# A sparse layer's experts, one at a time or two to a block, in a transformer layer on one core

## The chip, the core and the metric

The kernel runs on one core of a Trainium2 chip. The metric is device time in microseconds (us) of one execution, and the kernel before took 3014.79 us (median of three runs, 3014.07 to 3015.65). A core has a matrix engine (PE, with its weight loads shown apart as PEld), a vector engine (DVE), an activation engine (ACT), a general engine (POOL) and a queue that only issues transfers (SP). PE multiplies a stationary operand, loaded into its 128 x 128 array, by a moving one that streams through, and writes to PSUM, eight banks of 512 floats on each of 128 partitions. DVE and ACT carry results from there to SBUF. Transfers run on 16 DMA engines. Each engine works through its own queue in order and waits on semaphores for the others.

## The reference, cut to what matters

```
x = L0_attn_x                          # (8, 1024, 256) float32, 8192 tokens
x = x + 0.5 * ffn(layernorm(x))
x = x + attention(layernorm(x))        # 16 heads of 16
x = x + 0.5 * ffn(layernorm(x))

def ffn(input):                        # E = 8 experts, C = 320 places, D = 256, H = 1024
    xf = input.reshape(N, D)
    eid = argmax(softmax(xf @ router_w + router_b))
    rank = (number of earlier tokens of the same expert)
    valid = rank < C
    buf[eid, rank] = xf                # where valid
    h = relu(einsum('ecd,edh->ech', buf, w1) + b1)
    y = einsum('ech,ehd->ecd', h, w2) + b2
    yov = relu(xf @ ow1 + ob1) @ ow2 + ob2
    return y[eid, rank] where valid, else yov
```

Each expert takes the first 320 tokens that choose it. All later ones go through one shared network of the same shape, ow1 and ow2. Everything is float32.

## The kernel before, in words

Both feed-forwards are an object of the class `Layer`. Routing (`route`, `places`) normalizes a batch, finds each token's expert and rank, and scatters its row into a DRAM buffer, `buf`: 8 x 320 rows for the experts, then all tokens past them. A row has 256 values and the token's number.

`blocks` (lines 427 to 488) then works on blocks of rows, one after the other. A block of an expert has 320 rows, held as tiles of 128, 128 and 64; a shared block has 512, four tiles. For each block:

- `load` (411) has the rows on their way from `buf` (`load_rows`, 402, on SP). POOL copies out the token numbers (416) and gathers each token's old value into `old` (419, an indirect transfer that POOL issues).
- `transposed` (192) turns rows to columns: two transposes a tile on PE into PSUM (199), and one copy by ACT of the whole (204).
- The hidden layer is computed transposed. The 1024 hidden units are eight groups of 128, taken two at a time into a tile of two PSUM banks (`big`, two such tiles). For each group two matmuls (445) have a piece of w1 stationary and the block's columns moving: 320 columns for an expert, 512 for a shared block. ACT evicts the first bank of the two with bias and relu (455), DVE the second (458).
- DVE adds the halved second bias to the old values (467).
- For each tile, eight matmuls (473) accumulate the output: a piece of the hidden layer (128 hidden units by n tokens) is stationary, w2's rows (128 x 256) move. For an expert's third tile n is 64, so half of the array's columns have work.
- DVE evicts it as y, half of the product plus old (480), and POOL scatters y to the tokens' places (483).

The next block's transposes stand ahead of the present block's last tile (470), so that ACT's copy lies beside that tile's matmuls.

`expert` (491) makes a block for `blocks`: it loads the expert's second bias, b2, to all partitions (496), has POOL halve it (497), calls `load`, and loads w1 (`wa`, 501) and w2 (`wb`, 502) on SP, 1 MB each. `wa`, `wb` and `bb` have two buffers, so an expert's weights load while the one before computes.

The order on PE, ACT and DVE is that in which the program is written (`manual_schedule`). The order on POOL and SP is made by the framework, and both queues run in order. The framework places waits where a tile's buffer is used again, and also where a new pool's tile lies in memory on an older pool's tile.

`feed_forward` (590) runs the stages: shared blocks beside routing, then the eight experts in a pool of their own (633), then further shared blocks. The first feed-forward has its last shared blocks run beside the first steps of attention, the second runs two shared blocks after the experts.

Attention runs between the two (`attention`, 703). Of it this matters: for two batches in turn, the values stand in the tiles `vp0` and `vp1` (742), 8768 bytes of every partition each, in which ones beside the values give the softmax's sums. They lie in the pool `const`, open for the whole kernel, and POOL fills both with ones at the kernel's start. `weigh` (964) multiplies them: for each of four heads one matmul with 32 stationary columns, written to its own 32 PSUM partitions, so each head has its own quarter of the array's columns.

Of the kernel before, what the change touches and what calls it, by code (L numbers as in the profile page):

```python
# [40 lines left out]
def macaron(  # L41
# [12 lines left out]
    def big(name):  # L54
        return psum["big"].tile([P, 1024], F32, tag="big", name=name)
# [27 lines left out]
    def load(name, src, shape, pool=const):  # L83
        t = pool.tile(shape, F32, tag=name, name=name)
        nc.scalar.dma_start(out=t, in_=src)
        return t
# [105 lines left out]
    def transposed(pool, tag, name, rows):  # L192

        width = sum(n for _, n in rows)
        ps = big(f"pt_{name}").rearrange("p (k c) -> p k c", k=KC)
        at = 0
        for r, n in rows:
            for k in range(KC):
                nc.tensor.transpose(  # L199
                    ps[:, k, at : at + n], r[:n, k * P : (k + 1) * P], ident[:n, :n]  # L200
                )
            at += n
        to = pool.tile([P, KC, width], F32, tag=tag, name=name)
        nc.scalar.copy(to, ps[:, :, :width])  # L204
        return to
# [35 lines left out]
    class Layer:  # L241
# [169 lines left out]
        def load(self, pool, name, at, count, weights, bias, after):  # L411

            rows, olds = self.rows.pop(at, None) or self.load_rows(pool, name, at, count), []
            ids = pool.tile([P, WIDE // P], I32, tag="ids", name=f"ids_{name}")
            for i, (r, n) in enumerate(rows):
                nc.gpsimd.tensor_copy(ids[:n, i : i + 1], r[:n, D : D + 1].bitcast(I32))
                old = pool.tile([P, D], F32, tag="old", name=f"old_{name}_{i}")

                nc.gpsimd.indirect_dma_start(
                    out=old[:n, :], out_offset=None, in_=self.old,  # L420
                    in_offset=bass.IndirectOffsetOnAxis(ap=ids[:n, i : i + 1], axis=0),
                    bounds_check=N - 1, oob_is_err=False,
                )
                olds.append(old)
            return name, rows, ids, olds, weights, bias, after

        def blocks(self, pool, those, late=False):

            those = iter(those)
            one, xnt = next(those, None), None
            while one is not None:
                name, rows, ids, olds, (wa, wb), bias, after = one
                width = sum(n for _, n in rows)
                if xnt is None:
                    xnt = transposed(pool, "xet", f"bT_{name}", rows)
                    yield
                following = None if late else next(those, None)
                hs = []  # L440
                for m in range(0, MC, 2):
                    ps = big(f"ph_{name}_{m}")
                    for i in range(2):
                        for k in range(KC):
                            nc.tensor.matmul(  # L445
                                ps[:, i * 512 : i * 512 + width],
                                lhsT=wa[:, k, (m + i) * P : (m + i + 1) * P],
                                rhs=xnt[:, k, :],
                                start=(k == 0),
                                stop=(k == KC - 1),  # L450
                            )
                        if i == 0:
                            yield
                    h = pool.tile([P, 2, width], F32, tag="he", name=f"h_{name}_{m}")
                    nc.scalar.activation(  # L455
                        h[:, 0, :], ps[:, :width], AF.Relu, bias=bias[:, m : m + 1]
                    )
                    nc.vector.tensor_scalar(  # L458
                        h[:, 1, :], ps[:, 512 : 512 + width], bias[:, m + 1 : m + 2], 0.0,
                        ALU.add, ALU.max,  # L460
                    )
                    hs += [h[:, 0, :], h[:, 1, :]]
                    yield
                if late:
                    following = next(those, None)
                for (_, n), old in zip(rows, olds):
                    nc.vector.tensor_tensor(old[:n, :], old[:n, :], after[:n, :], ALU.add)
                for i, ((_, n), old) in enumerate(zip(rows, olds)):
                    if following is not None and i == len(rows) - 1:
                        xnt = transposed(pool, "xet", f"bT_{following[0]}", following[1])  # L470
                    ps = acc(f"pe_{name}_{i}")
                    for m in range(MC):
                        nc.tensor.matmul(  # L473
                            ps[:n, :D], lhsT=hs[m][:, i * P : i * P + n], rhs=wb[:, m, :],
                            start=(m == 0), stop=(m == MC - 1),
                        )
                        if m == MC // 2:
                            yield
                    y = pool.tile([P, D], F32, tag="y", name=f"y_{name}_{i}")
                    nc.vector.scalar_tensor_tensor(  # L480
                        y[:n, :], ps[:n, :D], 0.5, old[:n, :], ALU.mult, ALU.add
                    )
                    nc.gpsimd.indirect_dma_start(
                        out=self.new.pop(0),
                        out_offset=bass.IndirectOffsetOnAxis(ap=ids[:n, i : i + 1], axis=0),
                        in_=y[:n, :], in_offset=None, bounds_check=N - 1, oob_is_err=False,
                    )
                    yield
                one = following

        def expert(self, pool, e):
            name = f"{self.f}_{e}"
            wa = pool.tile([P, KC, H], F32, tag="wa", name=f"wa_{name}")
            wb = pool.tile([P, MC, D], F32, tag="wb", name=f"wb_{name}")
            bb = pool.tile([P, D], F32, tag="bb", name=f"bb_{name}")
            nc.sync.dma_start(out=bb, in_=b2[e].partition_broadcast(P))
            nc.gpsimd.tensor_scalar(bb, bb, 0.5, None, ALU.mult)
            one = self.load(
                pool, f"e{name}", e * CAP, CAP, (wa, wb), b1_sb[:, e * MC : (e + 1) * MC], bb
            )  # L500
            nc.sync.dma_start(out=wa, in_=w1[e].rearrange("(k p) f -> p k f", p=P))
            nc.sync.dma_start(out=wb, in_=w2[e].rearrange("(m p) d -> p m d", p=P))
            return one
# [86 lines left out]
        def feed_forward(self, start, others=None, following=None):  # L590
# [13 lines left out]
            with self.pools, space(f"ffn{f}", {  # L604
                "he": 4, "old": 8, "xet": 2, "y": 4
            }, self.main, side="right") as main:
                def past(at, width=WIDE):
                    return self.load(
                        main, f"o{f}_{at}", SLOTS + at, width, self.shared, ob1_sb, ob2_sb
                    )  # L610
# [9 lines left out]
                with two_sizes(f"ps{f}", 4):  # L620
# [12 lines left out]
                    with space(f"experts{f}", {"wa": 2, "wb": 2, "bb": 2}, main, side="right") as pool:  # L633
                        with tc.manual_schedule(engines=ordered):
                            end = at if f == 0 else sure(B - 1)
                            run(self.blocks(main, chain(
                                (self.expert(pool, e) for e in range(E)),
                                (past(i * WIDE) for i in range(at, end)),
                            )))
# [63 lines left out]
    def attention(use, kept, weights, router):  # L703
# [36 lines left out]
        for i in range(2):  # L740
            vp = kept.tile([P, TB * HEADS * V + S], F32, tag=f"vp{i}", name=f"vp{i}")
            nc.gpsimd.memset(vp, 1.0)
            vps.append(vp)
# [366 lines left out]

        def zero_rows(i):
            m = use.pool.tile([P, 512], F32R, tag=f"m{i}", name=f"m{i}")
            nc.gpsimd.memset(m.bitcast(F32), 0.0)
            ms.append(m)

        def first_pair(others):
# [4 lines left out]
            for i in range(2):  # L1121
                zero_rows(i)
            zero = clearing(use.pool)
# [36 lines left out]
        def run(own):  # L1160
            for i in range(2, 4):
                zero_rows(i)
            fetch(1)
            for b in range(AHEAD - 1, B):
                reload(b)
                beside.append([G * (b - 1) - 1, DVE, stats(b)])
# [74 lines left out]
    first_pair, run = attention(use, const, weights, layers[1])  # L1241

    def beside_last(blocks, main):
# [12 lines left out]
        "q0": 1, "k0": 1, "m0": 1, "m1": 1, "zero": 1, "lowest": 2, "lowboth": 2,  # L1256
# [3 lines left out]
    with space("early", sizes) as early:  # L1260
        layers[0].feed_forward(0, fill_weights, beside_last)
        own = {
            "ex": 8, "ho": 4, "xn": 4, "xnt": 1, "q1": 1, "q2": 1, "k1": 1, "k2": 1, "ot0": 1,
# [82 lines left out]
```

## Time and profile before

| what | value |
|---|---|
| median of three runs | 3014.79 us |
| profiled execution, its own time | 3016.21 us |
| its span, first to last instruction | 3014.3 us |
| PE, DVE, ACT, POOL busy | 94%, 62%, 45%, 29% |
| first experts, hidden layer's first matmul to the next block's transposes | 375.6 to 535.0 us |
| second experts, likewise to the next block's hidden layer | 2785.6 to 2945.9 us |
| granted PE clock, mean | 0.988 |

The profile is one execution. Its views are the page (busy time; the span in 40 slices with a digit for the tenths busy; the chain that ended last; groups of instructions), a timeline of each engine's instructions with equal ones merged, a table of busy time by stretches of time, and the waits. A matmul of float32 stands in the trace as two passes, so the counts of matmuls are twice the program's. Passes overlap in the pipeline: what a pass costs is the distance from its start to the next start, and not its duration. In a timeline's line the columns are start, length, engine, line, operation, output<-inputs, shape and count, and in brackets the idle time before it.

### The profile page before, as it was taken

The page shows a single profiled execution, that of the slowest core. Times are in us where ns is not written, and L with a number is a line of the kernel's source. Part 1 is how long each engine was busy: PE and PEld are TensorE (multiplying, and loading weights), DVE is VectorE, ACT ScalarE, POOL GpSimd, SP SyncE. Part 2 cuts the span into 40 slices and gives each one's busy share as a digit, 9 for nine tenths or more (in the row PEclk, how much of TensorE's full clock was granted, in tenths as well). Part 3 has the DMA queues.
Part 4 walks back from the last instruction along what each step waited for, and adds up shares of the span by engine and source line. Part 5 has one row for each costly group of instructions (what it writes and reads, how often), then busy time and mean ns, then how long its engine had stood idle before and what let it go on. Part 6 is the DMA issues. An engine that isn't in the chain of part 4 may idle for free.

```text
span 3014.3 us, 56661 instructions
## 1 busy us (share of the span) xinstructions
PE 2846.8 (94%) x22082; PEld 1570.5 (52%) x22082; DVE 1873.6 (62%) x4155; ACT 1367.9 (45%) x2480; POOL 878.0 (29%) x1176
## 2 busy tenths in 40 slices
PE   4599999999999999999999999999999998999998
PEld 4367677554444444444444444444444445667775
DVE  5344322366898788788788788788788953222221
ACT  0011111203766765766766766766766762111110
POOL 2353443513200121421421421421410215433331
PEclk9899999999999999999999999999999999999999
DMA  8241364423211211311311311311321102311430
GB/s 216 87 125 60 98 196 126 142 80 123 93 45 38 107 45 38 121 45 38 121 45 38 121 45 38 121 45 38 121 80 38 38 3 71 124 59 54 153 123 28
DMA packets 162840, 250.41 MB, mean 83 GB/s; under 512 B 36865, under 2 KB 108802, under 8 KB 162562
## 3 DMA queue, kind: packets, MB, share of 16 engines
q1 hardware_dynamic: 143026, 195.88, 20.1%
q0 software_dynamic: 18688, 50.62, 5.0%
q8 instruction: 177, 2.90, 0.4%
q14 instruction: 101, 0.83, 0.1%
q10 hardware_dynamic: 848, 0.18, 0.0%
HBM read 143.05 MB, written 103.57 MB: 82 GB/s over the span
## 4 chain that ended last, share of the span: by engine, by line
PE 62%; DVE 13%; issue 1%; POOL 1%; DMA 0%; ACT 0%; POOLq 0%; ACTq 0%
PE psc L933 19%; PE av L964 14%; DVE halves L949 9%; PE pm L933 6%; PE pe_o L473 5%; PE ph_o L445 5%; PE pe_e L473 3%; PE ph_e L445 2%; PE pu L1009 2%; PE pxd L808 2%; PE pv L840 1%; DVE turned L979 1%; PE pq L826 1%; PE pl L1037 1%; PE ptrn L778 0%
## 5 line engine op out<-in xcount | busy, mean ns | idle before, releaser
L949 DVE TENSOR_REDUCE halves<-pm 128x1 f32<-128x512 f32 x2048 | 1308.8, 681 | 255.7 <-PE pm L933 232.4
L942 ACT ACTIVATE ex<-psc 128x512 f32<-128x512 f32 x2048 | 1111.7, 596 | 572.4 <-PE psc L933 566.7
L933 PE MATMUL pm<-k,q 32*128 32x512 f32 x4096 | 870.3, 448 | 49.6 <-DVE halves L949 38.7
L933 PE MATMUL psc<-q,k 32*128 32x512 f32 x4096 | 790.1, 454 | 3.3 <-PEq L615 3.3
L964 PE MATMUL av<-ex,vp 128*32 128x256 f32 (+1 forms) x6472 | 610.1, 448 | 0.0
L933 PEld LDWEIGHTS psc<-q,k 32*128 32x128 f32 x4096 | 326.2, 183 | 478.9 <-issue 423.3
L933 PEld LDWEIGHTS pm<-k,q 32*128 32x128 f32 x4096 | 374.8, 183 | 133.1 <-DVE halves L949 108.6
L933 PE MATMUL psc<-m,ones_r 32*128 32x512 f32 x2048 | 406.5, 390 | 0.0
L445 PE MATMUL ph_o<-bT_o,oa 128*128 128x512 f32 x704 | 325.3, 613 | 10.9 <-DVE h_o L458 7.5
L473 PE MATMUL pe_o<-ob,h_o 128*128 128x256 f32 x1408 | 324.7, 387 | 0.0
L987 POOL TENSOR_TENSOR ot<-turned,rec 128x256 f32<-128x256 f32 x64 | 39.7, 621 | 881.7 <-DVE rec L982 875.4
L473 PEld LDWEIGHTS pe_o<-ob,h_o 128*128 128x128 f32 x1408 | 268.4, 194 | 47.6 <-issue 12.9
L964 PEld LDWEIGHTS av<-ex,vp 128*32 128x32 f32 x6472 | 127.6, 108 | 297.7 <-issue 274.9
L458 DVE TENSOR_SCALAR h_o<-ph_o,ob 128x512 f32<-128x512 f32 x88 | 66.0, 750 | 253.1 <-ACT h_o L455 235.3
L445 PEld LDWEIGHTS ph_o<-bT_o,oa 128*128 128x128 f32 x704 | 133.8, 195 | 167.4 <-issue 154.1
L455 ACT ACTIVATE h_o<-ph_o,ob 128x512 f32<-128x512 f32 x88 | 60.4, 687 | 332.2 <-PE ph_o L445 264.1
L933 PEld LDWEIGHTS psc<-m,ones_r 32*128 32x128 f32 x2048 | 196.0, 184 | 12.3
L473 PE MATMUL pe_e<-wb,h_e 128*128 128x256 f32 (+1 forms) x768 | 171.7, 380 | 0.0
L480 DVE SCALAR_TENSOR_TENSOR y_o<-pe_o,old_o 128x256 f32<-128x256 f32 x88 | 37.3, 423 | 184.2 <-PE pe_o L473 158.8
L473 PEld LDWEIGHTS pe_e<-wb,h_e 128*128 128x128 f32 (+1 forms) x768 | 131.0, 172 | 34.0 <-issue 0.5
L445 PE MATMUL ph_e<-bT_e,wa 128*128 128x320 f32 x512 | 142.1, 436 | 1.6 <-issue 0.8
L204 ACT COPY bT_o<-pt_bT_o 128x1024 f32<-128x1024 f32 x22 | 22.3, 1013 | 260.5 <-PE pt_bT_o L199 260.5
(173 smaller groups left out, 2364.0 us busy)
## 6 DMA issues: line engine op xcount, KB each, us to landing
k<-krows SPq DMA_DIRECT2D x64, 512.0 KB
wa<-in_w_dram SPq DMA_DIRECT2D x16, 1024.0 KB
wb<-in_w_dram SPq DMA_DIRECT2D x16, 1024.0 KB
krows<-kh SPq DMA_DIRECT2D x32, 512.0 KB
krows<-kl SPq DMA_DIRECT2D x32, 512.0 KB
q<-qrows SPq DMA_DIRECT2D x32, 512.0 KB
rows_o<-buf SPq DMA_DIRECT2D x88, 130.0 KB
x<-in_x_dram SPq DMA_DIRECT2D x8, 1024.0 KB
```

Source lines behind the costliest of these rows:

```text
L445: nc.tensor.matmul(ps[:, i * 512 : i * 512 + width], lhsT=wa[:, k, (m + i) * P : (m + i + 1) * P], rhs=xnt[:, k, :], start=(k == 0), stop= ...
L455: nc.scalar.activation(h[:, 0, :], ps[:, :width], AF.Relu, bias=bias[:, m : m + 1])
L458: nc.vector.tensor_scalar(h[:, 1, :], ps[:, 512 : 512 + width], bias[:, m + 1 : m + 2], 0.0, ALU.add, ALU.max,)
L473: nc.tensor.matmul(ps[:n, :D], lhsT=hs[m][:, i * P : i * P + n], rhs=wb[:, m, :], start=(m == 0), stop=(m == MC - 1),)
L480: nc.vector.scalar_tensor_tensor(y[:n, :], ps[:n, :D], 0.5, old[:n, :], ALU.mult, ALU.add)
L808: nc.tensor.matmul(ps, lhsT=wd_sb[:, k, m * P : (m + 1) * P], rhs=xnt[:, k, :], start=(k == 0), stop=(k == KC - 1),)
L933: nc.tensor.matmul(ps, lhsT=lhs, rhs=rhs, start=(len(left) + 1 == todo[kind, h, "of"]), stop=not left,)
L942: nc.scalar.activation(ex, ps, AF.Exp, scale=S ** -0.5)
L949: nc.vector.tensor_reduce(halves[m][:, t, half, h : h + 1], ps, AX.X, ALU.max, negate=True)
L964: nc.tensor.matmul(avs[n, q][32 * h : 32 * h + 32, cols], lhsT=vps[b % 2][:, at : at + 2 * S], rhs=ex[:, cols], start=(c == 0), stop=(c == ...
L987: nc.gpsimd.tensor_tensor(outs_t[q][:, :, at : at + S].rearrange("p (t a) s -> p a t s", t=4), by[:, :, :S].rearrange("p (a t) s -> p a t ...
L1009: nc.tensor.matmul(ps[:, i * D : (i + 1) * D], lhsT=outs[b, g, q][:, at : at + P], rhs=wu_sb[:, g, :], start=(g == 0), stop=(g == G // 2 - 1),
```

## The change

Two experts make one block of 640 rows, held as five full tiles. Its middle tile has the first expert's last 64 rows and the second's first 64. For every hidden group the middle tile gets two matmuls of 64 stationary columns: the first expert's, with the first w2, to PSUM partitions 0 to 63, and the second's, with the second w2, to 64 to 127.

- The hidden layer is computed expert by expert, as before. The first expert's is evicted in two pieces: columns 0 to 255 into h, and the last 64 into a new tile, `kept`, as the middle tile is computed after the second expert's hidden layer.
- Order in a block: first hidden layer, additions to five olds, tiles 0 and 1, second hidden layer, the middle tile, tile 3, next transposes, tile 4.
- `transposed` works in chunks of four tiles, each with a `big` of its own and a copy by ACT, so a pair has two copies, of 1024 and 256 elements.
- The second biases of a pair are one tile of three columns of 256 (first, both by halves, second), filled by four loads, with one buffer, halved by one instruction. `old` has 10 buffers instead of 8. `wa` and `wb` keep two buffers, one for each expert of the pair.
- `vp0` moves from `const` to the pool `early` and `vp1` to attention's own pool. Each is filled with ones by POOL there, `vp0` with attention's first steps, `vp1` as attention begins in earnest.

The diff, cut to its core:

```
     def transposed(pool, tag, name, rows):
+        to = pool.tile([P, KC, sum(n for _, n in rows)], F32, tag=tag, name=name)
         at = 0
+        for c in range(0, len(rows), 4):
+            ps = big(f"pt_{name}").rearrange("p (k c) -> p k c", k=KC)
+            width = 0
+            for r, n in rows[c : c + 4]:
+                for k in range(KC):
+                    nc.tensor.transpose(
+                        ps[:, k, width : width + n], r[:n, k * P : (k + 1) * P], ident[:n, :n]
+                    )
+                width += n
+            nc.scalar.copy(to[:, :, at : at + width], ps[:, :, :width])
+            at += width
         return to
...
+                for wa, wb, bias, (c0, c1) in parts:
+                    width = c1 - c0
+                    ahead = c1 % P if c1 != parts[-1][3][1] else 0
+                    if ahead:
+                        kept = pool.tile([P, MC, ahead], F32, tag="kept", name=f"kept_{name}")
...
+                        h = pool.tile([P, 2, width], F32, tag="he", name=f"h_{name}_{c0}_{m}")
+                        pieces = [(h, c0, c1 - ahead)]
+                        if ahead:
+                            pieces.append((kept[:, m : m + 2, :], c1 - ahead, c1))
+                        for t, lo, hi in pieces:
+                            nc.scalar.activation(
+                                t[:, 0, : hi - lo], ps[:, lo - c0 : hi - c0], AF.Relu,
+                                bias=bias[:, m : m + 1],
                             )
+                            nc.vector.tensor_scalar(
+                                t[:, 1, : hi - lo], ps[:, 512 + lo - c0 : 512 + hi - c0],
+                                bias[:, m + 1 : m + 2], 0.0, ALU.add, ALU.max,
+                            )
+                        for i in range(2):
+                            hs[m + i] += [(t[:, i, :], wb, lo, hi) for t, lo, hi in pieces]
...
+                    while to_do and to_do[0] * P + rows[to_do[0]][1] <= c1:
+                        i = to_do.pop(0)
+                        n = rows[i][1]
+                        if following is not None and not to_do:
+                            xnt = transposed(pool, "xet", f"bT_{following[0]}", following[1])
+                        ps = acc(f"pe_{name}_{i}")
+                        for m in range(MC):
+                            for of, w, a, b in hs[m]:
+                                lo, hi = max(i * P, a), min(i * P + n, b)
+                                if lo < hi:
+                                    nc.tensor.matmul(
+                                        ps[lo - i * P : hi - i * P, :D],
+                                        lhsT=of[:, lo - a : hi - a],
+                                        rhs=w[:, m, :],
+                                        start=(m == 0),
+                                        stop=(m == MC - 1),
+                                    )
...
+        def ones(i):
+            vp = use.pool.tile([P, TB * HEADS * V + S], F32, tag=f"vp{i}", name=f"vp{i}")
+            nc.gpsimd.memset(vp, 1.0)
+            vps.append(vp)
```

## The prediction

> **What bounds the kernel now.** The page's busy table and its slices come first.
>
> ```profile
> PE 2846.8 (94%) x22082; PEld 1570.5 (52%) x22082; DVE 1873.6 (62%) x4155; ACT 1367.9 (45%) x2480; POOL 878.0 (29%) x1176
> ...
> PE   4599999999999999999999999999999998999998
> PEld 4367677554444444444444444444444445667775
> DVE  5344322366898788788788788788788953222221
> ```
>
> PE is busy nearly everywhere, and outside attention (the tenth to the 34th slice) nothing else is near full. The edited code is a stage of its own, in the sixth and seventh slice and again in the 38th and 39th, where DVE is at 2 tenths. The table by stretches of time gives its two runs:
>
> ```profile
> 375.60:535.00 159.40, 159.40 (x682) 118.35 (x682) 35.28 (x79) 21.71 (x39) 64.30 (x86) 1.00 0.50 157
> 2785.60:2945.90 160.30, 160.30 (x691) 119.31 (x691) 35.27 (x79) 22.73 (x40) 58.92 (x81) 1.00 0.43 137
> ```
>
> PE is busy for the whole of both (first and second number equal), at full clock; DVE works 35 us of 159, ACT 22, and DMA is half used. So only PE's own work counts here. PE's timeline shows one expert:
>
> ```profile
> 475.66 8.88 PE L445 MATMUL ph_e<-bT_e,wa 128*128 128x320 f32 x32
> 484.38 7.07 PE L473 MATMUL pe_e<-wb,h_e 128*128 128x256 f32 x32
> 491.28 0.87 PE L199 MATMUL pt_bT_e<-ident,rows_e 128*128 128x128 f32 x6
> 492.08 3.67 PE L473 MATMUL pe_e<-wb,h_e 128*64 128x256 f32 x16
> 495.68 0.54 PE L445 MATMUL ph_e<-bT_e,wa 128*128 128x320 f32 x1
> ```
>
> Durations overlap, so I take differences of starts. Each matmul of the program stands as two passes in the trace (x16 for the eight of a tile). The hidden layer takes 484.38-475.66 = 8.72 us; two full tiles 6.90 (3.45 each, 0.2156 a pass); the next expert's transposes 0.80; the half tile 3.60, as long as a full one. Sum 20.02, eight times over.
>
> **The change part by part**, made against the profiled execution (3016.21 us, span 3014.3), which stands 1.4 us above the median of the runs, 3014.79; I subtract the difference from the median.
>
> *Unchanged:* the hidden layers, 8 x 8.72 a feed-forward, and 16 full tiles of 3.45 (two of each expert before; four of each pair after): 124.96 us.
>
> *The middle tile.* Before, eight half tiles a feed-forward, 28.8 us. After, four middle tiles, each with the same 32 passes of 64 columns, but alternating between the left and the right half of the array. The trace has no such pair. The nearest row is attention's, where four groups of 32 columns get a matmul each:
>
> ```profile
> 1505.66 0.40 PE L933 MATMUL psc<-m,ones_r 32*128 32x512 f32 x2
> 1505.99 0.64 PE L964 MATMUL av<-ex,vp 128*32 128x256 f32 x8
> 1506.56 0.50 PE L933 MATMUL psc<-q,k 32*128 32x512 f32 x2
> ```
>
> Eight passes of the half tile's length fill 0.57 us to the next start; one after the other they would need 8 x 0.2156 = 1.72. The records show four starting within 0.02 us, the other four 0.240 later. All four groups write one bank and use all 128 rows, as the two halves will. So two halves should run side by side: 16 steps of 0.2156 (the half tile's pass) to 0.240 (attention's), plus what entering and leaving 64 columns costs now, 3.60-16x0.2156 = 0.15. That is 3.60 to 3.99; I take 3.75, nearer the half tile, whose width and length it has. Four: 15.0 us, a gain of 13.8 a feed-forward (12.8 to 14.4).
>
> *Transposes.* In the stage's first run, seven experts' of 0.80 (5.6 us), in the second also 0.96 of the shared block that follows. The 64-row ones cost more than full ones: the full ones start 0.11 apart, the small pair takes the last 0.36. After: ten full ones for three pairs, 3 x 1.10 = 3.3, and in the second run 0.88 (eight full ones ahead of a full tile at 2581.51). Gains 2.3 and 2.4.
>
> *Entry.* A stage's first block has no tile to hide its transposes:
>
> ```profile
> 373.93 0.87 PE L199 MATMUL pt_bT_e<-ident,rows_e 128*128 128x128 f32 x6
> 374.38 4.13 SPq L407 DMA_DIRECT2D rows_e<-buf  x1
> 374.84 0.69 ACT L204 COPY bT_e<-pt_bT_e 128x640 f32<-128x640 f32 x1 [13.83 <-PE pt_bT_e L199]
> 375.58 1.61 PE L445 MATMUL ph_e<-bT_e,wa 128*128 128x320 f32 x5 [0.78 <-issue]
> ```
>
> That is 1.65 us from transposes to hidden layer. With eight transposes and a copy of 1024 it is 2.20 (535.01 to 537.21); a second copy, of 256, costs about 0.37 by the line through 0.69 (640) and 1.01 (1024), if the matmul waits for it. Loss 0.55 to 0.92 a stage, taken as 0.75. Inside the stage the two copies (1.4 us) lie beside a full tile of 3.45.
>
> *Evictions.* The first expert's hidden layer is now evicted in four pieces, and in the new program each waits for the one before: ACT 256, DVE 256, ACT 64, DVE 64 columns. From 527 and 687 ns (ACT, 320 and 512) and 550 and 750 (DVE), the pieces are about 0.47, 0.48, 0.31 and 0.28; with 0.20 from PE to ACT and three hand-overs of 0.03, 1.83 us. The other bank pair's matmuls cover 2.18 (a quarter of 8.72), so the cost is nothing, with 0.35 us to spare. If pieces ran as long as the 320 ones, the chain would be 2.45, and two waits of 0.27 in a pair would cost 4 us in all.
>
> *Loads and queues.* With a pair at 36 us, the last weights freed with time pressing are the first expert's wb: free after the middle tile (28 us in), needed 9 us into the next pair, 17 us later. Behind that wait on SP stand the next rows, whose transposes are a pair away. A megabyte took 3.6 us at the 292 GB/s of the stretch 375.6 to 395.6. The bias tile has one buffer and four loads, free after the additions (12 us in) and needed at 45. POOL has five gathers and five scatters of 1.3 us and a scaling of 2.7 in 36. In the first pair two more row loads stand ahead of wa, 0.5 us of SP each; 8.9 us lay between wa's issue (366.70) and its first use (375.58). Cost nothing.
>
> *DVE* makes 8 additions and 8 evictions of y fewer a feed-forward; it is idle there, gain nothing.
>
> *Attention's values.* Two memsets (3.79 us of POOL at 11.9, before PE's first matmul at 20.64, which waits for DVE) become one there and one at attention's start, 1.92 us ahead of POOL's an, which ended at 727.3 while PE took it at 732.75. Nothing, or a gain of up to 0.3 at the start. Tiles move in memory, so a wait for an older tile's reader may appear or go: the one of 7.54 us on PE at 2522.9 (ACT's second h_o behind the sends) stays, as both tiles keep their places; for others I allow 2 us either way.
>
> Sum: (13.8+2.3-0.75) + (13.8+2.4-0.75) = 30.8. 3014.8-30.8 = **2984 us**; with the bounds 2980 to 2990.
>
> **The rivals.**
> *Loads exposed.* If a pass's weight load hid only behind passes of other rows, each of the 16 steps would pay it: 0.137 (the 128*64 load's row). The middle tile would be 16x0.353+0.15 = 5.8, 2.05 more, 16.4 over eight: 3000. Against it: in the half tile the next load starts 2 ns after the pass before and the passes stay 0.2156 apart; in attention the second four loads start 0.03 us after the first passes. The Trainium skill, "TensorE: Matmul & The Clock Gate", in Part 3 on packing small matmuls, says that a weight load overlaps running matmuls only when its row group differs, and both halves use every row. By that rule the time is this rival's 3000; these rows speak against it.
> *Halves one after the other*, so that the edit doesn't do what it says: 32x0.2156+0.15 = 7.05, 3.3 more a pair, 26.4 in all: 3010. Attention's row speaks against it, but with 32 columns and a single round, never sixteen.
> *Slower.* Alternating halves run in turn and each also waits for its load: 32x0.353+0.15 = 11.4 a pair, 7.7 more, 61 in all: 3045. Its place is the middle tile, and it decides from 7.6 us of middle tile (0.233 a pass), where the gain of 3.85 a pair is used up. The first rival's rows and attention's both speak against it.
>
> **How the numbers follow.** Side by side 0.80 (2984, own range 2980 to 2990), loads exposed 0.08 (3000), in turn 0.06 (3010), slower 0.04 (3045); 0.02 for a late transfer or a new wait, of either sign. 0.2% is 6 us, about what a measurement of this kernel can tell from no change. The third rival (-4) lies within it. Faster 0.88, same 0.07, slower 0.05. The range, 2979 to 3000, takes in the forecast's and reaches to the first rival.
>
> **What would show it.** Per pair, PE's timeline should have 17.4 us of hidden layer, four full tiles of 3.45, one stretch of 128*64 passes of 3.6 to 4.0 with starts in twos, and ten transposes 0.11 apart, 36.1 in all against 40.0, with PE busy throughout and attention's stretch as long as before. A middle stretch of 5.8, 7 or 11 names the rival. A PE idle ahead of ph_e waiting for DVE would show my chain of evictions too short; one waiting for wa or wb, the slack of loads.

## The result, and the profile after

The changed kernel took 2984.6 us (median of four runs, 2979.6 to 2990.4) beside 3014.4 for the kernel before: a ratio of 0.9902, 95% interval 0.9883 to 0.9921. The forecast was 2984. The profiled execution is the fastest of the four, 2979.6 us with a span of 2977.9 at a mean granted clock of 0.989.

The same lines of the page as before, now of the changed kernel: PE's row of the busy table, then the slices.

```profile
PE 2814.6 (95%) x22066; PEld 1551.4 (52%) x22066; DVE 1875.2 (63%) x4171; ACT 1375.1 (46%) x2512; POOL 861.5 (29%) x1144
...
PE   4599999899999999999999999999999998999998
PEld 4367677555444444444444444444444444676775
DVE  4344322476898798788788788788788963222221
```

PE has 32.2 us less to do (2846.8 before) and is as full as it was; DVE and ACT have more instructions, not fewer. The table by stretches of time gives the two stages of the experts, to be laid beside 159.40 and 160.30:

```profile
368.80:511.55 142.75, 142.74 (x670) 108.68 (x671) 35.87 (x87) 25.11 (x55) 54.69 (x68) 1.00 0.53 173
2766.30:2909.95 143.65, 143.62 (x678) 109.54 (x679) 35.87 (x87) 26.14 (x56) 51.14 (x64) 1.00 0.47 152
```

Each stage is 16.65 us shorter, at full clock, and PE is busy in all of it (142.74 of 142.75 us in the first, 143.62 of 143.65 in the second): nothing new waits inside. ACT works 3.4 us more, for the extra pieces, and DVE 0.6, as the extra pieces outweigh the additions and evictions saved; neither shows in the length. PE's timeline has one pair of experts:

```profile
404.85 8.78 PE L454 MATMUL ph_e<-bT_e,wa 128*128 128x320 f32 x32
413.46 7.07 PE L497 MATMUL pe_e<-wb,h_e 128*128 128x256 f32 x32
420.37 8.78 PE L454 MATMUL ph_e<-bT_e,wa 128*128 128x320 f32 x32
429.07 0.43 PE L497 MATMUL pe_e<-wb,kept_e 128*64 128x256 f32 x1
429.08 0.43 PE L497 MATMUL pe_e<-wb,h_e 128*64 128x256 f32 x1
429.34 0.38 PE L497 MATMUL pe_e<-wb,kept_e 128*64 128x256 f32 x1
429.35 0.38 PE L497 MATMUL pe_e<-wb,h_e 128*64 128x256 f32 x1
429.56 0.38 PE L497 MATMUL pe_e<-wb,kept_e 128*64 128x256 f32 x1
429.56 0.38 PE L497 MATMUL pe_e<-wb,h_e 128*64 128x256 f32 x1
...
436.24 1.25 PE L201 MATMUL pt_bT_e<-ident,rows_e 128*128 128x128 f32 x10
437.33 3.62 PE L497 MATMUL pe_e<-wb,h_e 128*128 128x256 f32 x16
440.78 1.51 PE L454 MATMUL ph_e<-bT_e,wa 128*128 128x320 f32 x5
```

By differences of starts: hidden layers 8.61 and 8.70, two full tiles 6.91, the middle tile and tile 3 together 436.24-429.07 = 7.17, ten transposes 1.09, tile 4 3.45. A pair takes 440.78-404.85 = 35.93 (two experts before: 40.04; forecast: 36.1). In the middle tile a pass of `kept` (the first expert's half) and one of `h` (the second's) start 0.007 apart; after a first step of 0.27 the next two follow every 0.2159 us (mean of 14 steps). From its first pass to tile 3's first it takes 3.604 to 3.605 in all eight pairs, for 32 passes that would need 6.9 one at a time. PEld's timeline at the same place shows both halves' loads lying over each other and over the passes that began at 429.34 and 429.35:

```profile
429.34 0.14 PEld L497 LDWEIGHTS pe_e<-wb,kept_e 128*64 128x64 f32 x1
429.35 0.14 PEld L497 LDWEIGHTS pe_e<-wb,h_e 128*64 128x64 f32 x1
```

Where the span went, by the starts of PE's instructions in the traces (us; the two experts' rows run from the first hidden matmul to the last tile's last pass, attention's from its first matmul of scores to its last, the shared blocks' from their transposes, 0.2 to 0.3 us after that last pass):

| stretch | before | before, a second profile | after | after, a second profile |
|---|---|---|---|---|
| start to PE's first instruction | 20.64 | 20.81 | 20.23 | 20.27 |
| first PE instruction to first hidden layer | 88.59 | 87.82 | 87.96 | 86.98 |
| shared blocks beside routing | 264.70 | 260.07 | 258.48 | 261.42 |
| entry, transposes to hidden layer (each of two) | 1.65 | 1.65 | 2.14 | 2.14 |
| first experts | 159.12 | 159.12 | 142.54 | 142.54 |
| shared blocks, to attention's first | 183.89 | 182.78 | 184.50 | 180.73 |
| attention | 1784.47 | 1791.96 | 1787.27 | 1784.39 |
| attention's last scores to the second experts' transposes | 280.55 | 279.60 | 280.86 | 279.46 |
| second experts | 160.00 | 160.00 | 143.41 | 143.41 |
| their last pass to the end | 68.77 | 68.85 | 68.18 | 67.75 |
| span | 3014.3 | 3014.6 | 2977.9 | 2971.5 |

The experts' stages repeat to 0.01 us in both kernels; the stages outside scatter by several us between profiles of one kernel. So the change's own part is 2 x 16.6 - 2 x 0.49 = 32.2 us, and what the medians show beyond or below that has to be told from the scatter.

### The profile page after: what moved, and what is told of

It is laid out like the page before. It is cut to its first block, busy times and chain, and to the rows that moved or that the text cites. A ratio compares the mean times of both kernels' runs of the same rounds, so it can differ in the third digit from the quotient of the medians.

```text
span 2977.9 us, 56683 instructions
## 1 busy us (share of the span) xinstructions
PE 2814.6 (95%) x22066; PEld 1551.4 (52%) x22066; DVE 1875.2 (63%) x4171; ACT 1375.1 (46%) x2512; POOL 861.5 (29%) x1144
## 3 DMA queue, kind: packets, MB, share of 16 engines
q1 hardware_dynamic: 144178, 196.93, 20.2%
## 4 chain that ended last, share of the span: by engine, by line
PE 63%; DVE 12%; issue 1%; POOL 1%; DMA 0%; ACT 0%; POOLq 0%; ACTq 0%
PE psc L981 19%; PE av L1012 15%; DVE halves L997 9%; PE pm L981 6%; PE pe_o L497 5%; PE ph_o L454 5%; PE pe_e L497 2%; PE ph_e L454 2%; PE pu L1057 2%; PE pxd L856 2%; PE pv L888 1%; DVE turned L1027 1%; PE pq L874 1%; PE pl L1085 1%; PE ptrn L826 0%
## 5 line engine op out<-in xcount | busy, mean ns | idle before, releaser
L497 PE MATMUL pe_e<-wb,h_e 128*128 128x256 f32 (+1 forms) x640 | 143.9, 381 | 0.0
L497 PEld LDWEIGHTS pe_e<-wb,h_e 128*128 128x128 f32 (+1 forms) x640 | 112.9, 179 | 16.4 <-issue 3.1
```

Source lines behind the costliest of these rows:

```text
L497: nc.tensor.matmul(ps[lo - i * P : hi - i * P, :D], lhsT=of[:, lo - a : hi - a], rhs=w[:, m, :], start=(m == 0), stop=(m == MC - 1),)
```

## The experiments

My theory: the halves run side by side because their passes stand next to each other in the order and on separate columns, and nothing else in the kernel answers. The rivals are that one of these two conditions isn't needed, that loads set the pace, and that a part of the gain or of a loss lies outside the experts.

**The changed kernel again, and the kernel before again.** No edit.

> The changed kernel as it is, timed in more rounds. My theory: the gain is the mechanism's 32 us less what the clock takes or gives, so the ratio should come out between 0.988 and 0.991 (2979 to 2988 us), with the pair of experts at 35.9 us whatever the time. The rival, that attention's stretch got longer by the change (1787.3 us against 1784.5 in the two profiles): the same stretch should again be 2 to 3 us longer than before's at an equal mean clock.

> The kernel before as it is, for a second profile of it. In equal classes of the mean clock the changed kernel's runs are some 35 us shorter, its experts' two stages 32.2. My theory: the other 3 us are the spread of the throttle between profiles and stages, so this profile's stretches outside the experts lie among those of the variants (87 us from the first PE instruction to the first hidden layer, 260 to 262 us of routing, 1784 to 1790 us of attention) and its experts' stages are again 159.1 and 160.0 us. The rival, that the change also shortens the time outside: this profile repeats 88.6 and 264.7 us.

The changed kernel came to 2977.0 us (six runs, 2973.2 to 2986.1) beside 3016.5 (19 runs, 3005.7 to 3026.8): a ratio of 0.9880, 0.9859 to 0.9901, at the lower edge of what was expected (the time is 2 us below it). Attention's stretch was 1784.39 here and 1791.96 in the second profile of before, so the 2.8 us by which it had grown are no more than two profiles of one kernel differ by, and no effect of the change is shown there. The second profile of before gives 260.07 for routing in place of 264.70, among the variants' 260 to 262, and the experts' 159.12 and 160.00 again.

Each run's mean granted clock is known to 0.001, and time follows it. Before's runs average 3017.8 at 0.987, 3014.9 at 0.988 and 3010.3 at 0.990; the changed kernel's 2979.7 at 0.988 and 2974.1 at 0.990. A straight line of time against clock, with one slope for all kernels of this set and a level for each, puts the changed kernel 36 us below before at an equal clock (standard error under 1). The stages account for 32.2, the shorter tail after the last expert for 0.9 (from the last pass of an expert to the span's end 68.2 to 67.7 in the variants, 68.8 and 68.9 before), and an earlier first instruction on PE for some 0.4 (at 20.2 to 20.7 us in the profiles with pairs, 20.6 to 20.8 in those without); why the last two moved is open. Some 3 us are left that no stage of the profiles pins down, since the scatter of routing and attention is larger than that.

**Attention's values alone,** in the kernel before.

```
-        for i in range(2):
-            vp = kept.tile([P, TB * HEADS * V + S], F32, tag=f"vp{i}", name=f"vp{i}")
-            nc.gpsimd.memset(vp, 1.0)
-            vps.append(vp)
...
+            ones(0)
...
+            ones(1)
```

> The kernel before with nothing but attention's values moved to the later pools. My theory: nothing, 0 with 2 us either way (2 us for waits on older tiles), so a ratio between 0.9990 and 1.0010; the experts' stretch keeps 159 to 160 us and attention's stretch its 1784 us. The rival, that the moved values cost the 2.8 us by which attention's stretch grew in the profile after: 3017 to 3018 us and attention near 1787.

3010.5 us (12 runs) beside 3016.5: 0.9990, 0.9977 to 1.0004, and by the line against the clock 0.7 us less than before, with a standard error of 0.6. The experts' stages keep 159.12 and 160.00, attention took 1786.45. The move costs nothing; a gain of about 1 us can't be excluded.

**One half after the other,** on the same columns.

```
-                        for m in range(MC):
-                            for of, w, a, b in hs[m]:
...
+                        pieces = [
...
+                        pieces.sort(key=lambda s: (s[1], s[0]))
+                        for at, (m, lo, hi, of, w, a) in enumerate(pieces):
```

Here `pieces` collects the tile's matmuls, each with its hidden group (`s[0]`) and its first column (`s[1]`); sorted by the column first, all of the first half come before the second's.

> The middle tile computes all eight matmuls of its first half, then all eight of its second half, on the same columns as in the changed kernel. My theory: the alternation is what lets the halves run side by side; the queue takes matmuls in order, so the first half's 16 passes run alone except where the two halves meet: 32 x 0.2155 + 0.15 = 7.05 us a middle tile, 3.4 more, 27 us in all, near 3011. The rival, that separate columns suffice and the engine reaches past waiting passes: 3.6 us a middle tile and 2984.

3002.8 us (six runs), 25.8 above the changed kernel in the same set, or 22.6 by the line against the clock; the ratio to before is 0.9950, 0.9929 to 0.9972. In the stages it is 10.56 us each, 2.64 a pair (a middle tile of 6.244), and not the 3.4 that strict order would give. PE's timeline:

```profile
394.68 3.02 PE L499 MATMUL pe_e<-wb,kept_e 128*64 128x256 f32 x13
397.32 0.43 PE L499 MATMUL pe_e<-wb,h_e 128*64 128x256 f32 x1
397.53 0.38 PE L499 MATMUL pe_e<-wb,kept_e 128*64 128x256 f32 x1
397.59 0.38 PE L499 MATMUL pe_e<-wb,h_e 128*64 128x256 f32 x1
397.75 0.38 PE L499 MATMUL pe_e<-wb,kept_e 128*64 128x256 f32 x1
397.81 0.38 PE L499 MATMUL pe_e<-wb,h_e 128*64 128x256 f32 x1
397.97 0.38 PE L499 MATMUL pe_e<-wb,kept_e 128*64 128x256 f32 x1
```

Twelve passes of the first half run alone. With the 13th the second half's first starts, though in the program three more of the first half stand ahead of it: it overtakes them. Four passes overlap, and 28 steps are left. So both theories were off: alternation matters, but the engine reaches past passes of the first half, a short way. That those were waiting for their columns is my reading. How short the way is, the next two tell. Each of the variants that follow was timed once, the last (transposed three and two) apart; one time can't tell 1 us here, so I judge them by their traces.

**In twos and in fours.** The key of the sort is `(s[0] // 2, s[1], s[0])` and `(s[0] // 4, s[1], s[0])`: two, or four, matmuls of one half, then as many of the other.

> The middle tile takes two matmuls (four passes) of the first half, then two of the second, and so on. With one half after the other the second half's first pass began beside the 13th of the first half's 16, so I read that PE has four passes beyond the running one at hand, and starts each as soon as its own columns are free. My theory: groups of four passes then overlap fully, 3.6 to 3.7 us. The rival, that only neighbours in the order overlap: one pass at each of seven changes, 32-7 = 25 steps, 5.4 us.

> As in twos, but four matmuls (eight passes) of one half, then of the other. My theory of four passes at hand: at each of the three changes between halves four passes overlap, 32 - 12 = 20 steps of 0.2155, 4.3 us and 0.2 more. The rival, that the engine reaches as far as it likes and one half after the other had another reason: 3.6. That only one change in a tile overlaps: 6.2.

In twos the middle tile takes 3.655 (2984.8 us), in fours 4.631 (2994.5 us). In twos the second half begins beside the first half's first pass, ahead of the three that stand before it in the program:

```profile
394.74 0.43 PE L499 MATMUL pe_e<-wb,kept_e 128*64 128x256 f32 x1
394.76 0.43 PE L499 MATMUL pe_e<-wb,h_e 128*64 128x256 f32 x1
```

The timeline in fours:

```profile
394.70 1.29 PE L499 MATMUL pe_e<-wb,kept_e 128*64 128x256 f32 x5
395.62 0.43 PE L499 MATMUL pe_e<-wb,h_e 128*64 128x256 f32 x1
...
396.32 0.59 PE L499 MATMUL pe_e<-wb,h_e 128*64 128x256 f32 x2
396.54 0.43 PE L499 MATMUL pe_e<-wb,kept_e 128*64 128x256 f32 x1
```

Again the other half begins beside the pass that has three of its own half behind it, the fifth of eight here, and at the next change it is the same with the halves exchanged. Twenty steps of 0.2159 and what entering and leaving cost (3.605 - 16 x 0.2159 = 0.151 in the changed kernel) make 4.47; the other 0.16 fit the 0.057 by which the halves are out of step after each of the three changes. A reach of four passes fits all three orders. All have matmuls of two passes, so whether the reach counts passes or matmuls isn't shown.

**Both halves on the same columns,** in alternation.

```
-                                        ps[lo - i * P : hi - i * P, :D],
...
+                                    ps[: hi - lo, :D],
```

> The middle tile's matmuls alternate as in the changed kernel, but both halves are written to columns 0 to 63, one sum over both (so the right half's rows of the middle tile lack their product: the computation is changed there). My theory: it is the separate columns that let two passes run at once, so the tile takes 32 x 0.2155 + 0.15 to 0.2 = 7.05 to 7.1 us, 3.45 more a pair, near 3010. The rival, that two passes of 64 columns overlap wherever they stand: 3.6 us.

Both products add up on the first 64 PSUM partitions, so this variant leaves out the right half's own result. The middle tile takes 7.051 us, as expected, 13.8 a stage more, and the one run took 3000.3 us, at a clock of 0.990. The timeline shows what the order alone brings:

```profile
394.24 0.65 PE L496 MATMUL pe_e<-wb,kept_e 128*64 128x256 f32 x2
394.73 0.59 PE L496 MATMUL pe_e<-wb,h_e 128*64 128x256 f32 x2
395.16 0.59 PE L496 MATMUL pe_e<-wb,kept_e 128*64 128x256 f32 x2
```

No two passes start together; after the first, starts are 0.216 apart. Separate columns are the other condition.

**Shorter passes,** 128 and 64 columns of w2 in a matmul of the middle tile.

```
+                            for c in range(0, D, D // 2):
+                                for m_, lo, hi, of, w, a in mids:
+                                    nc.tensor.matmul(
+                                        ps[lo - i * P : hi - i * P, c : c + D // 2],
...
```

`mids` has the two matmuls of one hidden group, the first half's and the second's. The code for 64 columns has `D // 4` in place of `D // 2`.

> Each matmul of the middle tile moves 128 columns of wb instead of 256, twice as many matmuls, the halves still in alternation: 32 steps of two passes, each pass half as long (0.108 us), with the same load of 64 columns (0.137 us) ahead of each. It asks how much room the loads have. My theory, that both halves' loads run at once and beside passes of the same rows: a step is the longer of pass and load, 0.137, and the tile 32 x 0.137 = 4.4 us. If the load's record is mostly latency, 3.6. The rival, that a load can't run beside a load of the other half: 32 x 0.274 = 8.8 us; and that it can't run beside a pass of its own rows: 32 x 0.245 = 7.8.

> Each matmul of the middle tile moves 64 columns of wb, four times as many matmuls: 64 steps of two passes of about 0.054 us, each with its load of 64 columns. With passes of 0.109 us the loads were hidden, though their records are 0.137 long. My theory: a load really occupies the array's columns for a time that now decides, about as long as a pass of 64 columns, so a step is 0.054 to 0.109 us and the tile 3.6 to 7.0 us, with the value nearer 3.6 the closer the load's rate is to one row of weights a cycle. The rival, that loads are free at any length: 3.6 exactly, as with passes twice as long. That issue or the queue becomes the bound: steps above 0.109 and the two halves no longer in pairs.

With 128 columns the steps are 0.109 and the tile 3.644 (2980.2 us); with 64 they are 0.0583 and the tile 3.882 (2978.8 us). Two steps of each:

```profile
396.29 0.27 PE L508 MATMUL pe_e<-wb,kept_e 128*64 128x128 f32 x1
396.30 0.27 PE L508 MATMUL pe_e<-wb,h_e 128*64 128x128 f32 x1
396.40 0.27 PE L508 MATMUL pe_e<-wb,kept_e 128*64 128x128 f32 x1
396.41 0.27 PE L508 MATMUL pe_e<-wb,h_e 128*64 128x128 f32 x1
```

```profile
396.93 0.22 PE L508 MATMUL pe_e<-wb,kept_e 128*64 128x64 f32 x1
396.93 0.22 PE L508 MATMUL pe_e<-wb,h_e 128*64 128x64 f32 x1
396.99 0.22 PE L508 MATMUL pe_e<-wb,kept_e 128*64 128x64 f32 x1
396.99 0.22 PE L508 MATMUL pe_e<-wb,h_e 128*64 128x64 f32 x1
```

My 0.137 for a step was wrong: the load's record is longer than what the load takes of the array. Two loads of 64 columns and two passes fit into 0.0583 us, so in the changed kernel, with 0.2159 a step, loads have over three times the room that they need. Whether at 0.0583 the load or the issue sets the pace (an exact quarter of 0.2159 would be 0.0540) these runs don't tell.

**A longer chain of evictions.** The kept columns are evicted twice.

```
-                        for t, lo, hi in pieces:
+                        for t, lo, hi in pieces + pieces[1:]:
```

> The first expert's kept columns are evicted twice, so that ACT and DVE each make three evictions a pair of chunks instead of two. My theory: in the changed kernel the chain (1.66 us in its trace from ACT's first start to DVE's last end, 1.85 with the hand-over from PE) fits into the 2.18 us in which PE computes the other bank pair, so it costs nothing; with two more pieces of 0.31 and 0.28 and their hand-overs it becomes 2.5 us, and PE waits about 0.3 us for a bank pair two times in a pair of experts: 0.6 a pair, 4.8 us in all, shown as PE idle ahead of ph_e in the first half of each block. The rival, that the pieces of different engines needn't wait for one another or that there are more banks than I think: no idle ahead of ph_e, 35.93 us a pair as before.

Each stage is 2.38 us longer (144.92 and 145.79), 0.595 a pair, 4.8 in all: the size expected (the one run took 2983.8 us). In the timeline each piece starts 0.03 to 0.04 after the end of the one before, whichever engine has it:

```profile
376.45 0.28 DVE L472 TENSOR_SCALAR kept_e<-ph_e,b 128x64 f32<-128x64 f32 x1 [0.38 <-issue]
376.76 0.31 ACT L468 ACTIVATE kept_e<-ph_e,b 128x64 f32<-128x64 f32 x1 [0.35 <-issue]
377.11 0.28 DVE L472 TENSOR_SCALAR kept_e<-ph_e,b 128x64 f32<-128x64 f32 x1 [0.38 <-ACT kept_e L468]
...
377.54 4.54 PE L454 MATMUL ph_e<-bT_e,wa 128*128 128x320 f32 x16 [0.36 <-issue]
```

PE waits until the last of the four kept pieces has ended at 377.39, and starts at 377.54. The pieces do wait for one another, and the cover that I counted on ends where I put it.

**Transposed three and two,** an attempt at a better version.

```
-        for c in range(0, len(rows), 4):
+        step = 3 if len(rows) > 4 else 4
+        for c in range(0, len(rows), step):
```

> The entry alone is changed: a block of five tiles is transposed three and two instead of four and one. My theory: the first hidden matmul waits only for the first copy, so the entry goes from 2.14 us to six transposes' stretch and a copy of 768, about 1.75, twice in the kernel: 0.8 us less, which the whole time can hardly show. The rival, that the first matmul waits for both copies (its operand reaches into the second for the second expert only): 2.14 or more, since the second copy, of 512, then ends later. Inside the stage nothing changes, both copies lie beside a full tile.

The entry falls from 2.14 to 1.71 us, as the first expert's columns are in the first copy and the hidden layer waits for that alone:

```profile
367.62 1.26 PE L202 MATMUL pt_bT_e<-ident,rows_e 128*128 128x128 f32 x10
...
368.47 1.29 ACT L206 COPY bT_e<-pt_bT_e 128x768 f32<-128x768 f32 x2 [13.78 <-PE pt_bT_e L202]
...
369.33 1.07 PE L455 MATMUL ph_e<-bT_e,wa 128*128 128x320 f32 x3 [0.45 <-ACT bT_e L206]
```

PE starts at 369.33, while ACT's second copy is still running (the two copies, merged in this line, last to 369.76). The time, 2979.6 us (six runs) beside the changed kernel's 2977.0, can't show 0.9 us, and by the line against the clock it is 0.3 more, with a standard error of 0.8. By the stages it is the better version, by 0.86 us.

## Why the prediction was right, point by point

- *What bounds it: right.* The stage of the experts follows PE's starts alone. ACT got 3.4 us of work more there and the stage still ended 16.65 us earlier.
- *The middle tile: right in kind, a little dear.* 3.605 against 3.75, at the bottom of 3.60 to 3.99. The step is the half tile's, 0.2159 in both kernels, and not attention's 0.240; the 0.15 besides is the half tile's too. Over eight tiles 1.2 us.
- *Transposes: right.* 1.09 a pair against 1.10.
- *Entry: the term that was mis-sized.* I let the hidden layer wait for both copies or nearly and took 0.75, from bounds of 0.55 to 0.92; it lost 0.49, because its operand, the first expert's 320 columns, lies in the first copy of 512. These lines of the changed kernel show it: the two copies, merged, run to 369.03, PE starts at 368.81.

```profile
366.67 1.25 PE L201 MATMUL pt_bT_e<-ident,rows_e 128*128 128x128 f32 x10
...
367.74 1.29 ACT L205 COPY bT_e<-pt_bT_e 128x1024 f32<-128x1024 f32 x2 [14.00 <-PE pt_bT_e L201]
...
368.81 1.61 PE L454 MATMUL ph_e<-bT_e,wa 128*128 128x320 f32 x5 [0.88 <-issue]
```

- *Evictions: right.* The timeline of all engines has the pieces at the durations that I drew from the larger ones, and the chain's end at 372.92, ahead of the next at 373.48:

```profile
371.26 0.47 ACT L468 ACTIVATE h_e<-ph_e,b 128x256 f32<-128x256 f32 x1 [2.24 <-issue]
371.77 0.48 DVE L472 TENSOR_SCALAR h_e<-ph_e,b 128x256 f32<-128x256 f32 x1 [4.48 <-ACT h_e L468]
...
372.29 0.31 ACT L468 ACTIVATE kept_e<-ph_e,b 128x64 f32<-128x64 f32 x1 [0.55 <-DVE h_e L472]
372.64 0.28 DVE L472 TENSOR_SCALAR kept_e<-ph_e,b 128x64 f32<-128x64 f32 x1 [0.38 <-issue]
```

  The slack of 0.35 us was real and as thin as stated: 0.65 us more of chain cost 0.3 a wait.
- *Loads, queues, DVE: right.* PE is busy for 142.74 of 142.75 us; no pair waits for wa or wb.
- *Attention's values: right,* by the experiment that moves them alone.
- *The rivals.* Loads exposed would have been 5.8 a middle tile; the changed kernel has 3.605, and the variant with four times as many loads 3.882. On weight loads the Trainium skill, "TensorE: Matmul & The Clock Gate", Part 3, says that a load overlaps running matmuls only when its row group differs. The traces disagree: here both halves use all rows, and the loads at 429.34 and 429.35 overlap the passes that began with them. Halves in turn, 7.05, is what the same columns give (7.051); on separate columns the slowest order tried still gives 6.24. (What the prediction calls its third rival, at -4, is halves in turn, its second.) The slower case, from 7.6 on, is out of reach of every variant.
- *The sum.* 30.8 forecast, 32.2 by the stages: 1.2 from the middle tile, 0.5 from the entries, and 0.3 less elsewhere. The median of the first four runs, 29.8 less than before, agrees with the forecast more closely than its working deserves; the second set gives 39.5. Both hold the stages' 32.2 and a few us that the clock gives or takes.

## What to carry to other kernels

Half-width matmuls that must be done anyway are worth pairing on the two halves of the array, if both halves' results can go to their own PSUM partitions and the program alternates them; groups of up to two matmuls of float32 (four passes) a side cost only 0.05 us of 3.6 more, longer groups lose. Price such a change by the distance from start to start of the passes, and check what the pairing adds to the chain that frees PSUM: here it fitted with 0.35 us to spare. Where the gain is 1% and the whole moves by 0.7% with the clock (3005.7 to 3026.8 us at 0.991 to 0.983, before), compare the edited stage, which repeated to 0.01 us, and not only the medians.

## What the runs showed of the hardware that was not expected

- PE starts passes out of the program's order. With one half after the other, the second half's first pass started at 397.32, ahead of three of the first half's that stand before it in the program (397.53, 397.75, 397.97). That those three had to wait for the first half's columns and could be passed is how I read it; the starts and the 2.64 us instead of 3.4 are what was measured. The reach was four passes in each order tried, with float32 alone.
- A load's record says little of what it costs: 0.137 us long, yet two loads and two passes fit into a step of 0.0583.
- The stages outside the experts differ by up to 7.5 us between two profiles of the same kernel (attention 1784.47 and 1791.96, before) at an equal mean clock of 0.988.
